# Reuse waits by tile, rope tables in a pool of their own, and gated weights fetched inside the attention, in a two-part transformer kernel

## The chip, the cores and the metric

The kernel runs on one core of a Trainium2 chip. Its time is the device time of one execution in microseconds. Engines are named as the profile names them: PE (TensorE, matrix products), PEld (its weight loads), DVE (VectorE), ACT (ScalarE), POOL (GpSimd), SP (SyncE, which here only issues DMAs). Each runs its own instructions in the order in which they were written down, and waits on the others by semaphores.

## The reference

Two residual sandwiches over x of shape 2 x 2048 x 256, in float32:

```python
x = x + layernorm(attn(layernorm(x)))   # compressed, selected and windowed attention, gated, 16 or so small products
x = x + layernorm(ffn(layernorm(x)))    # two layers, below

# one layer of ffn, 8 heads of 64, window 128
h = shift_token(x)                      # second half of the channels taken from the token before
q, k, v = split(h @ wqkv)
q, k = l2norm(q) * qs, l2norm(k) * ks
q, k = rotary_xpos(q, k)                # multiply by tables of cos and sin times a scale per position
x = x + local_attention(q, k, v) @ wo   # each block of 128 sees itself and the block before
h = layernorm(shift_token(x)) * lg + lb
a, g = split(h @ w1 + b1)
x = x + (a * gelu(g)) @ w2 + b2
```

## The kernel before, in words

The tokens are 32 tiles of 128 rows. Tensors X and Y hold them in SBUF throughout. **Part one** computes the first sandwich. Its instructions are noted down first and then given out in an order written out by hand (`FIRST`; line 150 of the profile is where they are given out). Its pools (`psum1`, `wa`, `big`, `work`, `tiny`) are then released. **Part two** computes the two layers. Each step is put on a list with a place, a number that stands for a due time in nanoseconds; the list is sorted by place and given out in that order (line 124 in the profile is the helper through which these instructions go). In both parts the order on each engine is the order of the program; nothing reorders it.

Pools of part two: `psum2` (PSUM banks, tags pa 2, pb 2, pc 4), `wf` (gated weights w1, w2, b2, the projection wo, the ring of keys KR, the inner activations U) and `act` (the tiles of the attention and of the gated stage). They are laid on the bytes and banks that part one's pools left. `wpool`, opened before part one's pools, holds wqkv and the scales qks; it takes over nothing.

The attention of a layer goes tile by tile, 32 tiles, alternating between the two sequences, 12,400 apart in place (`TILE`), each with 46 or so steps at fixed offsets (`PLACES`). The steps that matter here, for tile n:

- `table_load` (offset -20000, SP): for every second tile one DMA of 128 KB, a rope table `cs`; three buffers.
- `turn_input` (0, PE), `late_half` and `early_half` (ACT copies to `h`), `edge` (1424, POOL).
- `project` j = 1, 0, 2 (2265, 5394, 10688, PE): keys, queries, values, each into a pa bank, of which there are two.
- `square` (ACT), `table` (4442, POOL: cs times qks), `times` (8622 and 9762, DVE: projections times table, tile `rr`), `values` (ACT).
- `add`, `power`, `unit` (11152 to 18200, POOL: rotation and normalisation of rr), then `turn` (19662 and 20098, PE).
- `scores` (21969 and 29455, PE), softmax, `weigh`, `project_out` (49850, PE, which reads wo).

The gated stage of a layer overlaps the end of its attention; its first use of w1, w2, b2 and U in layer one is some 640 us into the span. `load_wo` issues one DMA on SP. `load_gated` issues a DMA on POOL (b2), a POOL memset, four DMAs on SP (w1), a second POOL memset, two DMAs on SP (w2); two of the w1 DMAs and the last w2 DMA write where a memset wrote. U's two tiles get a memset each on POOL.

In the kernel before, `fetch(0, "wo")`, `fetch(0, "gated")` and U's memsets stand ahead of the whole list, so they are the first instructions of part two on SP and POOL:

```python
    W[0]["wqkv"], W[0]["qks"] = attn_w
    fetch(0, "wo")
    fetch(0, "gated")
    begin = 0
```

Of the kernel before, what the change touches and what calls it, by code (L numbers as in the profile page):

```python
# [10 lines left out]
F32 = mybir.dt.float32  # L11
# [5 lines left out]
P = 128  # L17
# [11 lines left out]
DEPTH, HEADS, DH = 2, 8, 64  # L29
INNER = HEADS * DH  # L30
HID = int(H * 4 * 2 / 3)
NCH = -(-HID // P)
# [121 lines left out]
def sandwich_kernel(ctx: ExitStack, tc: tile.TileContext, x, Wq, bq, Wk, bk, Wv, bv, Wo, bo, Wg, bg,  # L154
                    Wc, bc, Ws, bs, wqkv, q_scale, k_scale, wo, ln_g, ln_b, w1, b1, w2, b2, rope, out):
    nc = Notes(tc.nc)
# [7 lines left out]

    def share(stack, name, **bufs):
        banks.update(bufs=bufs, pool=stack.enter_context(
            tc.tile_pool(name=name, bufs=1, space=bass.MemoryType.PSUM)))

    def bank(tag, shape):
        return later(banks["pool"], shape, F32, tag=tag, name=tag, bufs=banks["bufs"][tag])  # L170
# [16 lines left out]

    part1 = ExitStack()
    share(part1, "psum1", pa=3, pb=2, pc=2, po=1)


# [72 lines left out]
    wpool = ctx.enter_context(tc.tile_pool(name="wpool", bufs=1))  # L264

    def load_wqkv(l):
        a = wpool.tile([P, 2, 3 * INNER], F32, tag="wqkv", name=f"wqkv{l}")
        nc.cut()
        nc.sync.dma_start(a, wqkv[l].rearrange("(h p) n -> p h n", p=P))

        v = wpool.tile([P, 2, 2, DH], F32, tag="qks", name=f"qks{l}")
        for i in range(2):
            for j, sc in enumerate((q_scale[l], k_scale[l])):
                nc.cut()
                nc.sync.dma_start(v[:, i, j, :], sc.unsqueeze(0).to_broadcast([P, DH]))
        return a, v
# [601 lines left out]


    share(ctx, "psum2", pa=2, pb=2, pc=4)  # L880
    wf = ctx.enter_context(tc.tile_pool(name="wf", bufs=1))
    act = ctx.enter_context(tc.tile_pool(name="act", bufs=2))

    def load_wo(l):
        wo_s = wf.tile([P, INNER // P, H], F32, tag="wo", name=f"wo{l}")
        nc.sync.dma_start(wo_s, wo[l].rearrange("(h p) n -> p h n", p=P))
        return wo_s

    def load_gated(l):
        b2_b = wf.tile([P, H], F32, tag="b2", name=f"b2{l}")  # L890
        nc.gpsimd.dma_start(b2_b, b2[l].unsqueeze(0).to_broadcast([P, H]))


        a = wf.tile([P, 2, W1C], F32, tag="w1", name=f"w1{l}")
        w1v = w1[l].rearrange("(h p) n -> p h n", p=P)
        nc.gpsimd.memset(a[:, :, 2 * FULL :], 0.0)
        nc.sync.dma_start(a[:, :, 0:FULL], w1v[:, :, 0:FULL])
        nc.sync.dma_start(a[:, :, FULL : 2 * FULL], w1v[:, :, HID : HID + FULL])
        nc.sync.dma_start(a[:, :, 2 * FULL : 2 * FULL + REST], w1v[:, :, HID + FULL : 2 * HID])
        nc.sync.dma_start(a[:, :, 2 * FULL + HALF : 2 * FULL + HALF + REST], w1v[:, :, FULL:HID])  # L900
        o = wf.tile([P, NCH, H], F32, tag="w2", name=f"w2{l}")
        nc.gpsimd.memset(o[:, NCH - 1, :], 0.0)
        nc.sync.dma_start(o[:, 0 : NCH - 1, :], w2[l, 0:FULL, :].rearrange("(c p) n -> p c n", p=P))
        nc.sync.dma_start(o[0:REST, NCH - 1, :], w2[l, FULL:HID, :])
        return a, o, b2_b
# [5 lines left out]
    def put(place, f, *args):  # L911
        todo.append((place, len(todo), f, args))
# [26 lines left out]
    def attention(l, base):  # L939
        tabs = {}  # L940
        S = [dict() for _ in ORDER]

        def table_load(n):

            t, b = ORDER[n]
            if b == 0:
                tabs[t] = act.tile([P, 2, 2, DH], F32, tag="cs", name="cs", bufs=3)
                nc.sync.dma_start(tabs[t], rope[:, t].rearrange("p (i j) d -> p i j d", i=2))

        def table(n):  # L950
# [237 lines left out]

    U = [wf.tile([P, NCH, GT * P], F32, tag=f"u{i}", name=f"u{i}") for i in range(2)]
    for u in U:  # L1190
        nc.gpsimd.memset(u[:, NCH - 1, :], 0.0)

    def gated_units(l, base, no_gate_until, beside):
        G = {g: dict(u=U[i % 2]) for i, g in enumerate(GORDER)}
# [107 lines left out]
    def fetch(l, what):  # L1302
        if what == "wqkv":
            W[l]["wqkv"], W[l]["qks"] = load_wqkv(l)
        elif what == "wo":
            W[l]["wo"] = load_wo(l)
        else:
            W[l]["w1"], W[l]["w2"], W[l]["b2"] = load_gated(l)
# [1 line left out]


    W[0]["wqkv"], W[0]["qks"] = attn_w
    fetch(0, "wo")
    fetch(0, "gated")
    begin = 0
    for l in range(DEPTH):
        last_tile = begin + (len(ORDER) - 1) * TILE
# [60 lines left out]
```

## Time and profile before

| what | value |
|---|---|
| median of 3 runs | 1618.66 us (1618.02 to 1618.82) |
| the profiled execution | 1617.42 us, span 1615.7 us |
| mean granted PE clock | 0.976 |
| PE busy | 1530.9 us, 95% of the span |
| DVE, ACT, POOL busy | 66%, 47%, 45% |
| part one ends (last ACT instruction) | 241.0 us into the span |
| attention of layer one, PE full | 300 to 640 us, 339.98 of 340 busy |

The granted clock is the share of full speed that PE was given; at 0.50 a projection of 4 matmul records takes 3.4 us, at 1.00 it takes 1.7. Windows cut the span into stretches and give the busy time of each engine in each. A wait "A <- B" is idle time of A that ended when B did something. The timeline lists instructions in order of time; SPq and POOLq are the queues' own instructions.

### The profile page before, as it was taken

Reading aid. Unit: us, or ns where it says so; the run is one execution under the profiler, and the core shown is the slowest. Engines: PE = TensorE matmul, PEld = TensorE weight load, DVE = VectorE, ACT = ScalarE, POOL = GpSimd, SP = SyncE. Lnnn points to the kernel's source line nnn. Section 1 sums busy time; section 2 is a strip of 40 time slices with the busy share of each in tenths; the row PEclk is TensorE's granted clock in tenths of the full one; section 3 lists DMA queues with packets and bytes.
Section 4 is the critical chain, followed back from the end, with each engine's and each line's share of the span. In section 5 each row is a group of like instructions: output and inputs, shape, how many; then the busy total and the mean of one; then the engine's idle time right before and its main releaser. Section 6 shows DMA issues by size and latency. Waiting matters only on the chain.

```text
span 1615.7 us, 32188 instructions
## 1 busy us (share of the span) xinstructions
PE 1530.9 (95%) x12216; PEld 1013.0 (63%) x12216; DVE 1068.0 (66%) x3123; ACT 757.3 (47%) x2197; POOL 733.5 (45%) x906
## 2 busy tenths in 40 slices
PE   7999957999999999789999999999999987999998
PEld 6867743666666666546566556666666664656655
DVE  6588673788888888544445247888888884455543
ACT  5236652677676776411111147677676763111110
POOL 7114255666666666301111156666666661132332
PEclk9999987999999999899999999999999998999999
DMA  6000002000000000020000010000000000000000
GB/s 213 1 4 4 1 2 80 8 5 8 6 8 9 5 7 7 8 68 7 10 20 0 1 39 28 9 5 9 5 8 8 9 4 9 11 25 28 27 26 26
DMA packets 32389, 30.66 MB, mean 19 GB/s; under 512 B 5118, under 2 KB 30572, under 8 KB 32236
## 3 DMA queue, kind: packets, MB, share of 16 engines
q1 hardware_dynamic: 32044, 28.08, 5.7%
q8 instruction: 97, 1.59, 0.4%
q0 software_dynamic: 192, 0.52, 0.2%
q14 instruction: 56, 0.46, 0.1%
HBM read 20.21 MB, written 4.19 MB: 15 GB/s over the span
## 4 chain that ended last, share of the span: by engine, by line
PE 87%; DVE 5%; POOL 3%; DMA 3%; ACT 1%; issue 1%; SPq 0%; POOLq 0%; DVEq 0%; ACTq 0%
PE pa L124 30%; PE pb L124 23%; PE pc L124 23%; PE pa L150 5%; PE pc L150 3%; DMA sh<-Y 2%; PE pb L150 2%; PE po L150 1%; DVE prob L124 1%; POOL rr L124 1%; DVE rr L124 1%; DVE st L150 1%; POOL r L150 1%; DMA cs<-in_rope_dram 0%; POOL ss L124 0%
## 5 line engine op out<-in xcount | busy, mean ns | idle before, releaser
L124 PE MATMUL pa<-wqkv,h 128*128 128x512 f32 x768 | 377.6, 615 | 19.3 <-ACT h L124 9.9
L124 POOL TENSOR_TENSOR rr<-rr 128x256 f32<-128x256 f32 x256 | 178.0, 727 | 305.8 <-DVE rr L124 259.4
L124 ACT ACTIVATE ge<-pa,vb 128x512 f32<-128x512 f32 x92 | 63.1, 688 | 365.7 <-PE pa L124 360.3
L124 ACT ACTIVATE prob<-prob,off 128x192 f32<-128x192 f32 (+2 forms) x512 | 226.2, 445 | 11.9 <-DVE off L124 11.0
L124 PEld LDWEIGHTS pa<-wqkv,h 128*128 128x128 f32 x768 | 133.9, 194 | 134.7 <-issue 107.7
L124 POOL TENSOR_TENSOR ss<-ss,mhalf 128x16 f32<-128x16 f32 x64 | 188.0, 2937 | 3.3 <-DVE den L124 2.3
L124 ACT COPY probT<-pb 128x384 f32<-128x384 f32 (+1 forms) x256 | 119.9, 469 | 142.6 <-PE pb L124 139.6
L124 PE MATMUL pa<-hh,w 128*128 128x512 f32 x368 | 176.4, 609 | 5.3 <-ACT ge L124 5.3
L124 PE MATMUL pc<-w,u 128*128 128x256 f32 x768 | 175.7, 379 | 0.0
L124 PEld LDWEIGHTS pc<-w,u 128*128 128x128 f32 x768 | 145.8, 190 | 45.4 <-issue 28.7
L124 DVE CUSTOM_DVE_ANT_0 prob<-pc,mask_loc 128x192 f32<-128x192 f32 (+2 forms) x512 | 148.7, 346 | 25.9 <-PE pc L124 24.1
L124 DVE TENSOR_TENSOR rr<-pa,cs 128x1024 f32<-128x1024 f32 x128 | 150.6, 1216 | 21.6 <-POOL cs L124 14.0
L124 PE MATMUL pb<-hh,w 128*128 128x512 f32 x292 | 137.7, 594 | 0.0
L124 POOL TENSOR_SCALAR r<-mv 128x1 f32<-128x1 f32 (+1 forms) x48 | 11.2, 233 | 274.9 <-DVE mv L124 274.9
L124 POOL TENSOR_TENSOR rr<-rr,ss 128x512 f32<-128x512 f32 x128 | 132.9, 1058 | 2.3
L124 DVE TENSOR_TENSOR prob<-prob,den 128x768 f32<-128x768 f32 x128 | 128.0, 1000 | 4.9
L124 PE MATMUL pb<-wo,oT 128*128 128x256 f32 x512 | 124.8, 388 | 5.8 <-DVE oT L124 5.8
L124 PEld LDWEIGHTS pb<-ident,prob 128*128 128x128 f32 x752 | 89.2, 141 | 65.4 <-DVE prob L124 27.7
L124 PE MATMUL pb<-ident,prob 128*128 128x128 f32 x752 | 118.3, 279 | 11.2 <-DVE prob L124 9.4
L124 DVE SCALAR_TENSOR_TENSOR u<-pb,vb,ge 128x512 f32<-128x512 f32 x73 | 54.7, 750 | 105.6 <-PE pb L124 79.8
L124 ACT ACTIVATE sq<-pa 128x512 f32<-128x512 f32 x128 | 75.9, 593 | 97.0 <-PE pa L124 94.2
L124 PE MATMUL pc<-kr,qT 64*64 64x192 f32 (+2 forms) x2688 | 111.1, 289 | 3.4 <-ACT qT L124 3.4
(255 smaller groups left out, 2498.6 us busy)
## 6 DMA issues: line engine op xcount, KB each, us to landing
cs<-in_rope_dram SPq DMA_DIRECT2D x32, 128.0 KB
out_dram<-res SPq DMA_DIRECT2D x32, 128.0 KB
sh<-Y SPq DMA_DIRECT2D x16, 254.0 KB
w<-in_L_ffn_w_dram SPq DMA_DIRECT2D x6, 640.0 KB
X<-_attn_hidden_states_dram SPq DMA_DIRECT2D x7, 512.0 KB
wqkv<-in_L_ffn_wqkv_dram SPq DMA_DIRECT2D x2, 1536.0 KB
Wc<-in_L_attn_Wc_dram SPq DMA_DIRECT2D x1, 1024.0 KB
wo<-in_L_ffn_wo_dram SPq DMA_DIRECT2D x2, 512.0 KB
```

The source lines that it names most:

```text
L124: return f(*a, **k)
L150: f(*(now(x) for x in a), **{n: now(x) for n, x in k.items()})
```

## The change

Three things. The pools `psum2`, `wf` and `act` (and `psum1`, by the shared helper) are opened with `reuse_waits="tile"`: a tile that lands on bytes of released pools waits for the users of the tiles that lay on its own bytes (in PSUM, on its own bank), where before every tile of the pool waited for every user of the released pools. The rope tables move from `act` to `wpool`, still with three buffers. The load of wo, the load of the gated weights and U's memsets are put on the list at places 12000, 60000 and 61000.

```diff
     def share(stack, name, **bufs):
         banks.update(bufs=bufs, pool=stack.enter_context(
-            tc.tile_pool(name=name, bufs=1, space=bass.MemoryType.PSUM)))
+            tc.tile_pool(name=name, bufs=1, space=bass.MemoryType.PSUM, reuse_waits="tile")))
...
-    wf = ctx.enter_context(tc.tile_pool(name="wf", bufs=1))
-    act = ctx.enter_context(tc.tile_pool(name="act", bufs=2))
+
+    wf = ctx.enter_context(tc.tile_pool(name="wf", bufs=1, reuse_waits="tile"))
+    act = ctx.enter_context(tc.tile_pool(name="act", bufs=2, reuse_waits="tile"))
...
-                tabs[t] = act.tile([P, 2, 2, DH], F32, tag="cs", name="cs", bufs=3)
+                tabs[t] = wpool.tile([P, 2, 2, DH], F32, tag="cs", name="cs", bufs=3)
...
-        nc.gpsimd.memset(u[:, NCH - 1, :], 0.0)
+        put(61000, nc.gpsimd.memset, u[:, NCH - 1, :], 0.0)
...
-    fetch(0, "wo")
-    fetch(0, "gated")
+    put(12000, fetch, 0, "wo")
+    put(60000, fetch, 0, "gated")
```

## The prediction

> **What bounds the kernel now.** I read the page first, then the windows over the hand-over from the first to the second part, then the waits there, then the timeline. The page says that TensorE is the bound:
>
> ```profile
> PE 1530.9 (95%) x12216; PEld 1013.0 (63%) x12216; DVE 1068.0 (66%) x3123; ACT 757.3 (47%) x2197; POOL 733.5 (45%) x906
> ```
>
> So only what shortens a hole in PE, or work done at half clock, can pay. From 300 to 640 us the windows give PE 339.98 of 340 us busy at clock 1.00: a time gained before 300 is kept to 640. The diff acts at the hand-over, so I cut that into 3.4 us slots (columns: stretch, length, busy of PE, PEld, DVE, ACT, POOL, then granted clock, DMA share, GB/s):
>
> ```profile
> 240.70:244.10 3.40, 2.57 (x3) 1.00 (x4) 0.00 (x0) 0.74 (x3) 2.20 (x6) 0.50 0.59 155
> 244.10:247.50 3.40, 3.40 (x5) 1.35 (x4) 0.00 (x0) 0.60 (x1) 0.00 (x0) 0.50 1.06 331
> 247.50:250.90 3.40, 0.74 (x2) 0.00 (x0) 0.00 (x0) 0.60 (x1) 0.00 (x0) 0.99 0.99 294
> 250.90:254.40 3.50, 0.00 (x0) 0.00 (x0) 0.56 (x1) 0.00 (x0) 0.72 (x1) 0.51 0.47 141
> 254.40:257.80 3.40, 2.68 (x3) 1.18 (x4) 3.28 (x4) 0.00 (x0) 1.52 (x3) 0.50 0.00 0
> 257.80:261.20 3.40, 2.88 (x6) 1.29 (x5) 0.00 (x0) 0.93 (x3) 3.40 (x4) 0.50 0.00 0
> 261.20:264.60 3.40, 3.40 (x5) 1.34 (x5) 0.29 (x1) 0.60 (x1) 2.81 (x3) 0.50 0.00 0
> 264.60:268.00 3.40, 2.62 (x27) 1.58 (x26) 2.37 (x3) 1.57 (x3) 0.13 (x1) 1.00 0.00 0
> ...
> 274.80:278.30 3.50, 1.89 (x10) 0.84 (x8) 3.18 (x4) 1.47 (x5) 2.66 (x4) 0.99 0.00 0
> 278.30:281.70 3.40, 2.86 (x20) 1.99 (x21) 2.06 (x3) 1.47 (x6) 2.74 (x5) 0.50 0.00 0
> ```
>
> Two things are to be seen. PE is empty from 248.2 to 255.1 while the DMA moves 300 GB/s. And the clock of a slot follows how full PE was in the slot before: 3.40 of 3.40 gives 1.00 next, 2.57 to 2.88 leaves 0.50 at 0.50, 1.89 of 3.50 drops 1.00 to 0.50. What PE waited for, from the waits of 240 to 300 us (total, times, longest):
>
> ```profile
> DVE rr L124 <- POOL cs L124: 14.0, 1, 14.0
> POOL cs L124 <- DMA cs<-in_rope_dram: 9.8, 1, 9.8
> PE pa L124 <- DVE rr L124: 6.9, 1, 6.9
> ```
>
> The third projection of tile 0 (`project`, part 2) needs a pa bank that `times` has to empty; `times` needs the table cs, scaled on POOL; the table needs its DMA. The timeline says why that is late:
>
> ```profile
> 241.03 0.38 SPq L124 DMA_DIRECT2D wo<-in_L_ffn_wo_dram  x1
> 241.04 0.44 ACT L124 COPY h<-pb 128x128 f32<-128x128 f32 x2
> 241.46 3.68 SPq L124 DMA_DIRECT2D w<-in_L_ffn_w_dram  x6
> 241.53 6.71 PE L124 MATMUL pa<-wqkv,h 128*128 128x512 f32 x8 [7.46 <-ACT h L124]
> 245.25 1.48 SPq L124 DMA_DIRECT2D cs<-in_rope_dram  x3
> ```
>
> SP issued its last load of part one at 32.5 and then waited 207 us for part one to end; only behind wo and six gated weights came the tables, which landed at 252.9.
>
> **The change, part by part.**
>
> *Waits by tile.* ACT runs in order and ends part one's last `Y<-X` at 241.01; the h copy follows at 241.04. So the wait by tile moves neither it nor PE's start at 241.53: gain 0. PE's first transposes may move from 233.38 to 232.7, under cover of that same wait: 0. POOL ends part one at 239.7; the edge memset (0.12) leaves 243.15 for 241.0 or earlier.
>
> *Tables in wpool.* They take over no old bytes, and at place -20000 and 4800 they stand ahead of wo: the first two are issued at about 33 us and have landed long before 241. The scaling (0.73) is done by about 241.9. `times` then waits for the square alone: the first runs 246.07 to 247.29 (square 245.44 + 0.60), the second 248.90 to 250.13 (square 248.28 + 0.60), instead of 253.84 to 256.20.
>
> *What is late next.* I replay the fill with the durations of the timeline:
> - PE: tile 0's third projection now at 247.9, at clock 1.00 (the full slot before it grants that), 4 x 0.43: to 249.65. Tile 1's transposes 0.38, copies and hand-over 0.6, its two projections 3.46: to 254.1.
> - POOL: from the end of `times` to the end of `unit` before is 256.20 to 264.09, 7.9 us (adds 2.77, power 2.92, units 2.04). Now 250.13 + 7.9 = 258.0, the first unit 1.0 earlier.
> - So PE has nothing from 254.1 to 257.0: **the hole shrinks and moves to `unit`**. That slot is a quarter full; the next runs at 0.50, and since it fills to about 80% the one after too. Slow: key and query turns to 259.05, qT copy, scores 259.75 to 260.95, values of tile 1 (3.4) to 264.35, transposes of tile 2 (0.64) to 264.95.
> - Fast again: tile 2's first projection 265.5 to 267.2, scores 0.65, second projection to 269.6, tile 1's turns to 270.5 (its units done at 267.9, not late), scores at 271.2, tile 2's values at 272.1, tile 3's first projection at 275.0. Before, that began at 285.05, after a slow stretch from 278.3 to 285.1 that now has no cause.
> - POOL is the limit once more: `times` of tile 2 ends at 273.3, and its units, which took 278.96 to 289.05 before with 1.4 us of waits in it, end at 273.4 + 8.8 = 282.2. PE ends tile 2's turns at 282.7 instead of 290.86: **8.1 us**. After this PE had no waits before and I expect none.
>
> *The clock rule.* The row comes first: 1.89 us of work in a 3.50 us slot was enough for 0.50 in the next, and a start at 241.53 became fast at 247.5 only. The Trainium skill, "TensorE: Matmul & The Clock Gate", Part 1 (The HAM clock gate), has the clock fall after at least one idle window of about 3.4 us. By that, a pause of 2.9 us costs nothing: values of tile 1 take 1.73 for 3.4, and the fill comes out at 10.8 us. I take the rows' 8.1.
>
> *Gated weights and u at 60000 and 61000.* On POOL the fetch is one b2 DMA (0.64) and two memsets of w (0.58 together); it falls behind tile 3's units (place 55400) and ahead of tile 4's adds (60752), where POOL waited 3.89 us:
>
> ```profile
> 299.75 2.05 POOL L124 TENSOR_TENSOR rr<-rr,ss 128x512 f32<-128x512 f32 x2
> 305.69 2.79 POOL L124 TENSOR_TENSOR rr<-rr 128x256 f32<-128x256 f32 x4 [3.89 <-DVE rr L124]
> ```
>
> 1.2 in 3.9: 0. The two u memsets (0.99) come between tile 4's adds; the units then end 1.0 later, where they had 0.8 to 0.9 us before PE's turns at 313.5 and 314.4: a loss of **0.2**. Uncovered, all 2.2 us would show. A rule that speaks against this: "SBUF — State Buffer", in "SBUF: two separate sides", has POOL fully blocked, descriptors for its DMAs too, while DVE runs a two-port operation. The trace's DMA issue took 0.642 beside an idle DVE and 0.647 in the second layer's attention, but DVE was idle for most of that one too, so the rows don't refute it. By the rule one DVE operation (up to 1.2, `rr`) more: 2.4 in 3.9, still 0; with a second one, 3.6, still inside.
>
> *SP's queue.* The gated weights' last pieces follow a POOL memset, so SP stands until about 292, and behind it the table of tile 8. That one is scaled at about 341 now (12.5 us a tile); 2.1 MB at the 300 GB/s seen are 7 us: 40 us to spare. wo, ahead of tile 4's table, waits till 241 at most; the table is needed near 290. Issuing costs PE nothing. The 2.1 MB now fall into full attention: in the second layer, with the DMA at 347 GB/s from 970 to 972, PE was 2.00 of 2.00 busy: 0.
>
> *More waits in instructions.* The trace doesn't show them; gaps of POOL's queue around its waits are 0.04 each. Below: 0, as they can be over before 241. Above: some twenty first uses of tiles between 241 and 282, 0.8 us. Taken: 0, nearest to what the copy at 241.04 shows, 0.03 after its predecessor.
>
> **Sum.** Profiled execution 1617.42 (span 1615.7 and 1.7 around it) - 8.1 + 0.2 = 1609.5. The median of the runs stands 1.24 above that execution; 1618.66 - 7.9 = 1610.76, said as **1610.7**.
>
> **Rivals.**
> - *The clock stays up* (the page's rule, or slots that fall otherwise): 10.8 gained less 0.2, 1608.1. For: a slot half full, 1.99 of 3.40 at 210, kept 1.00. Against: the 1.89 above.
> - *More slow slots*: each costs 1.7 us, half of 3.4. Two more in the fill or at 640 to 720: 1614.1. For: the slots' edges fall elsewhere once the work is shifted.
> - *The change doesn't do what it says*: the waits by tile could be ignored for some pool. The tables would still be early, in a pool that takes over nothing, so 1610.7 stands; only if SP still held them behind old users would it be 1618.7.
> - *Slower*: the layer change (640 to 720) and the start of the last gated stage (1330 to 1390) each hold about five slow slots, 17 us, with fast ones between. A shift of 8 us moves their edges. With 1.7 us a slot, 7 more than before turn the gain into a loss of over 0.2%: 8 more give 1624. Against: full slots restore the clock by themselves.
>
> **How the numbers follow.** The likeliest 0.68; clock stays up 0.10; more slow slots 0.10; no effect 0.04; slower 0.08. The first three are faster by over 0.2% (3.2 us, about what a measurement of this kernel can tell): 0.88; same 0.04; slower 0.08. The likeliest one's own range is 1608.5 to 1613; with clock and slots on both sides 1606.5 to 1615.0, which leaves out no effect, slower and a little.
>
> **What would show it.** Tables issued near 33 us; `times` of tile 0 beginning near 246.1 with no wait for cs; PE's hole before its third projection gone, one of about 3 us before tile 0's turns; tile 3's first projection near 275; tile 2's turns done near 282.7; the six w loads near 291. Wrong if PE starts part two away from 241.5, if POOL's chain is not what PE waits for, or if a wait appears between 290 and 640.

## The result

| | before | after |
|---|---|---|
| median of 5 runs each, same chip | 1618.66 us (1615.83 to 1619.02) | 1610.11 us (1607.32 to 1610.5) |
| profiled execution, its span | 1617.42, 1615.7 us | 1610.34, 1608.6 us |
| mean granted PE clock | 0.976 | 0.980 |
| PE busy | 1530.9 us | 1525.9 us |

The ratio is 0.9947, with an interval of 0.9932 to 0.9961: 8.55 us less. It was 1610.7 that was forecast. The change was timed again later (e10 below): 0.9966 (0.9955 to 0.9977), 5.0 us. Why the gain itself moves is one of the findings below.

The bound is the same; the first two lines of the page after:

```profile
span 1608.6 us, 32178 instructions
...
PE 1525.9 (95%) x12216; PEld 1012.2 (63%) x12216; DVE 1068.5 (66%) x3123; ACT 754.7 (47%) x2197; POOL 734.9 (46%) x906
```

SP's queue after (start, duration, operation, count; a row with a long duration holds a wait):

```profile
31.33 1.00 SPq L124 DMA_DIRECT2D cs<-in_rope_dram  x2
225.96 0.38 SPq L124 DMA_DIRECT2D wo<-in_L_ffn_wo_dram  x1
226.38 32.54 SPq L124 DMA_DIRECT2D cs<-in_rope_dram  x2
258.97 35.55 SPq L124 DMA_DIRECT2D w<-in_L_ffn_w_dram  x6
```

The first two tables are issued 200 us before they are used, and the gated weights no longer stand at the hand-over.

The waits after, from 240 to 300 us (total, times, longest). The three lines that the prediction showed are gone; these stand in their place:

```profile
POOL rr L124 <- DVE rr L124: 17.8, 4, 9.3
...
DVE rr L124 <- ACT sq L124: 10.4, 4, 6.2
...
PE pb L124 <- POOL rr L124: 2.8, 4, 1.1
...
PE pa L124 <- POOL h L124: 1.4, 2, 0.9
```

`times` (DVE rr) now waits for the square alone, and no wait of PE on POOL is longer than 1.1 us. The windows after, over the same stretches as in the prediction (columns as there):

```profile
240.70:244.10 3.40, 0.81 (x1) 0.50 (x2) 0.71 (x1) 2.01 (x5) 0.94 (x3) 0.50 0.00 0
244.10:247.50 3.40, 3.40 (x6) 1.38 (x5) 0.00 (x0) 0.39 (x1) 0.00 (x0) 0.54 0.00 0
247.50:250.90 3.40, 3.23 (x8) 1.17 (x7) 2.54 (x3) 0.81 (x2) 0.00 (x0) 1.00 0.00 0
250.90:254.40 3.50, 2.12 (x7) 0.80 (x6) 1.45 (x2) 0.92 (x3) 3.45 (x6) 1.00 0.00 0
254.40:257.80 3.40, 2.26 (x7) 0.71 (x5) 1.72 (x2) 1.19 (x2) 3.32 (x3) 1.00 0.00 0
257.80:261.20 3.40, 2.33 (x25) 1.54 (x26) 2.79 (x8) 1.17 (x2) 3.40 (x5) 1.00 0.38 93
...
278.30:281.70 3.40, 2.12 (x17) 1.01 (x19) 2.85 (x4) 1.66 (x6) 2.59 (x4) 1.00 0.00 0
```

The empty stretch is gone, and from 247.2 to 650 the clock stays at 1.00, where before six slots of the fill ran at 0.50. But PE starts part two later than before, as the timeline of the hand-over after shows:

```profile
240.92 0.73 POOL L124 TENSOR_TENSOR cs<-cs,qks 128x256 f32<-128x256 f32 x1
240.95 0.71 DVE L150 SCALAR_TENSOR_TENSOR CLOSE<-mv,CLOSE 128x2 f32<-128x2 f32 x1 [0.89 <-POOL h L124]
241.69 1.09 ACT L150 ACTIVATE Y<-X,CLOSE 128x256 f32<-128x256 f32 x2 [0.51 <-DVE CLOSE L150]
242.81 0.43 ACT L124 COPY h<-pb 128x128 f32<-128x128 f32 x2
...
243.29 5.62 PE L124 MATMUL pa<-wqkv,h 128*128 128x512 f32 x8 [8.89 <-ACT h L124]
...
247.81 1.23 DVE L124 TENSOR_TENSOR rr<-pa,cs 128x1024 f32<-128x1024 f32 x1 [6.16 <-ACT sq L124]
```

Part one's last CLOSE on DVE takes 0.71 us; the one before it took 0.16. It ends at 241.66 with POOL's table product at 241.65, which the free table has let in there. The last `Y<-X`, the copy and PE follow it.

**Where the 7 us of the profiled pair came from.** Both kernels issue the same 12,216 PE matmul records in the same order, so the start of the n-th can be subtracted (my arithmetic on the traces, each counted from the start of its own span, as the timelines are; the first profile of before is the zero). The table has this for all runs. "Start" is the first projection of part two, "fill" the gain from there to the scores right behind tile 2's turns, "U" the loss from there until after U's memsets, "rest" everything later. "End" is the last matrix product; it differs from the zero as the spans do. Minus is earlier, in us.

| run | start | fill | U | rest | end |
|---|---|---|---|---|---|
| after | +1.76 | -11.13 | +1.06 | +1.23 | -7.08 |
| e1 tables only | +2.28 | -10.91 | +0.07 | +2.15 | -6.42 |
| e2 order only | -0.27 | -10.92 | +1.06 | +1.42 | -8.71 |
| e3 waits by tile only | -0.26 | -9.39 | +0.07 | +2.02 | -7.57 |
| e4 U early | +0.12 | -11.06 | +0.07 | -1.36 | -12.24 |
| e5 edge early | +0.22 | -9.02 | +0.92 | +2.31 | -5.56 |
| e6 no waits by tile | +1.48 | -11.01 | +1.06 | +1.31 | -7.16 |
| e7 order, U early | -0.35 | -11.00 | +0.06 | -1.28 | -12.57 |
| e8 units delayed | -0.30 | -7.92 | +0.07 | -0.30 | -8.45 |
| e10 change again | -0.14 | -9.77 | +1.06 | -0.90 | -9.75 |
| e11 U early again | +1.76 | -10.31 | +0.07 | +2.52 | -5.95 |
| e12 no waits, U early | -0.28 | -10.85 | +0.06 | +2.06 | -9.01 |
| e13 before again | +1.18 | -3.47 | -0.01 | +0.97 | -1.33 |

### The profile page after: what moved, and what is told of

The parts are those of the page before. It is cut to its first block, busy times and chain, and to the rows that moved or that the text cites. A ratio compares the mean times of both kernels' runs of the same rounds, so it can differ in the third digit from the quotient of the medians.

```text
span 1608.6 us, 32178 instructions
## 1 busy us (share of the span) xinstructions
PE 1525.9 (95%) x12216; PEld 1012.2 (63%) x12216; DVE 1068.5 (66%) x3123; ACT 754.7 (47%) x2197; POOL 734.9 (46%) x906
## 4 chain that ended last, share of the span: by engine, by line
PE 74%; DVE 4%; POOL 2%; DMA 2%; ACT 1%; issue 1%; SPq 0%; POOLq 0%; DVEq 0%; ACTq 0%
PE pa L124 28%; PE pb L124 23%; PE pc L124 22%; DMA sh<-Y 2%; DVE prob L124 2%; POOL rr L124 1%; DVE rr L124 1%; POOL ss L124 1%; ACT prob L124 0%; DVE hh L124 0%; DVE st L124 0%; DVE ss L124 0%; DVE Y L124 0%; ACT L124 0%; DVE oT L124 0%
## 5 line engine op out<-in xcount | busy, mean ns | idle before, releaser
L124 PE MATMUL pa<-wqkv,h 128*128 128x512 f32 x768 | 371.6, 606 | 16.5 <-ACT h L124 11.6
L124 POOL TENSOR_SCALAR r<-mv 128x1 f32<-128x1 f32 (+1 forms) x48 | 11.1, 232 | 276.1 <-DVE mv L124 276.1
```

Of the source, the lines that this page charges most:

```text
L124: return f(*a, **k)
```

## The experiments

Diffs are against the changed kernel unless said otherwise. The first four ran on one chip beside the kernel before at 1616.32 us, the next four beside 1617.13, the next three beside 1614.05, the last beside 1615.44. Two theories stood at the outset: that SP's order (the gated load out of the way) gives the gain, or that the tables' buffers, which take over nothing, give it by themselves.

**e1, the tables alone.** Waits by tile off, fetches and U's memsets back ahead of the list:

```diff
-    put(12000, fetch, 0, "wo")
-    put(60000, fetch, 0, "gated")
+    fetch(0, "wo")
+    fetch(0, "gated")
```

> Only the tables move to wpool; waits by pool, and wo and the gated weights stay first on SP. Theory (the first table is late because it stands behind wo and six gated loads in SP's queue): SP still stands until 241, the tables are issued near 245, PE's hole before tile 0's third projection stays at about 6.9 us, time 1618.7 within 1.5. Rival (buffers that take over nothing are what counts): tables near 33 us, about 1610.

Measured 1608.25 us, 0.9956 (0.9941 to 0.9971): the theory missed, the full gain is there. SP's queue in this kernel:

```profile
31.25 1.42 SPq L124 DMA_DIRECT2D cs<-in_rope_dram  x3
243.31 0.38 SPq L124 DMA_DIRECT2D wo<-in_L_ffn_wo_dram  x1
243.74 4.06 SPq L124 DMA_DIRECT2D w<-in_L_ffn_w_dram  x6
```

In the program's text the fetches come first, in the trace the tables do, 212 us ahead of them. So the section on the kernel before is wrong where it says that nothing reorders part two. The order written out for part one and the list of part two stand inside `with tc.manual_schedule()` in the kernel; the two fetches stand outside both, and here they came out behind the three free tables. Nothing else moved: PE, DVE, ACT and POOL have the order of the kernel before, instruction for instruction. As an edit, the buffers that take over nothing are enough. But e1 changed SP's order too; what free tables gain behind waiting loads was not run.

**e2, the order alone.** Fetches and memsets at 12000, 60000 and 61000; tables in `act`, no waits by tile:

```diff
-                tabs[t] = wpool.tile([P, 2, 2, DH], F32, tag="cs", name="cs", bufs=3)
+                tabs[t] = act.tile([P, 2, 2, DH], F32, tag="cs", name="cs", bufs=3)
```

> Only the order moves (wo at 12000, gated weights at 60000, u at 61000); tables stay in act, all pools wait as before. Theory (SP's order is the cause): the table is issued at 241.0 as SP's first, lands near 244 and is scaled by 245, ahead of the square's end at 246.1; the whole gain, 1609 to 1611.5. Also DVE's last CLOSE step of part one keeps its 0.16 us, since POOL's table product comes later. Rival (waits by tile are what frees the start): no gain, 1618.7.

Measured 1608.43, 0.9954 (0.9941 to 0.9967), as the theory had it. The tables are SP's first issue of part two, at 240.77, and POOL has one early enough:

```profile
243.45 0.72 POOL L124 TENSOR_TENSOR cs<-cs,qks 128x256 f32<-128x256 f32 x1 [2.55 <-DMA cs<-in_rope_dram]
```

`times` needs it at 245.77, when the square is done: 1.6 us to spare. Either part gives the whole gain; together they give it once.

**e3, the waits by tile alone.** All pools by tile; tables in `act`, fetches and memsets first.

```diff
-        put(61000, nc.gpsimd.memset, u[:, NCH - 1, :], 0.0)
+        nc.gpsimd.memset(u[:, NCH - 1, :], 0.0)
```

> Only the three pools wait by tile; order and tables as before. Theory: SP can issue wo and the first gated loads once their own bytes are free, some 15 us earlier, but the last four gated loads follow POOL's memsets, which come behind part one's last POOL step, both u memsets and the b2 DMA (240 + 2.2), so the tables are issued near 244.3 and land near 247; times begins near 248 instead of 246.1: about 2 us of the gain missing, 1612 to 1613.5. Rival (waits by tile are all of it): 1610. Rival (waits do nothing alone): 1618.7.

Measured 1610.88, 0.997 (0.9962 to 0.9978), 5.4 us less where the theory had 5.2 to 6.7. wo goes out at 224.82, but the six gated pieces hold SP until 243.50, and POOL gets the table late:

```profile
247.51 0.72 POOL L124 TENSOR_TENSOR cs<-cs,qks 128x256 f32<-128x256 f32 x1 [5.93 <-DMA cs<-in_rope_dram]
```

`times` begins at 248.26, and the fill gains 9.39 instead of some 11. The waits help in this order of SP; they aren't the best way. Of the changed versions e3 alone keeps SP's order, with the tables behind the gated loads; in e1, e2 and the change the tables stand ahead of them, and the fill gains 10.9 to 11.1. So it is their place in SP's queue that the full gain goes with.

**e4, U's memsets ahead of the adds.**

```diff
-        put(61000, nc.gpsimd.memset, u[:, NCH - 1, :], 0.0)
+        put(56000, nc.gpsimd.memset, u[:, NCH - 1, :], 0.0)
```

> The changed kernel with u's two memsets at 56000 instead of 61000, so that they fall into POOL's idle gap ahead of tile 4's adds. Theory: the step of 1.05 us by which PE falls back between 300 and 307 us is the memsets between the adds; it goes, and PE's wait for the edge step there with it; 1609.1. Rival: the memsets cost about 1 us wherever they stand in the attention, 1610.1.

Measured 1606.31, 0.9945 (0.9927 to 0.9963). In the change the memsets cut tile 4's adds in two. Its timeline:

```profile
297.75 0.97 POOL L124 MEMSET u<- 128x512 f32 x2
...
298.70 1.40 POOL L124 TENSOR_TENSOR rr<-rr 128x256 f32<-128x256 f32 x2
...
299.97 0.96 DVE L124 TENSOR_TENSOR prob<-prob,den 128x768 f32<-128x768 f32 x1
300.05 0.93 POOL L124 COPY h<-h 128x1 f32<-128x1 f32 x1
...
301.03 1.13 PE L124 MATMUL pa<-wqkv,h 128*128 128x512 f32 x2 [0.45 <-POOL h L124]
```

The adds end late, the edge copy behind them falls beside a DVE multiply and takes 0.93, and PE waits for it; the rest comes with the units, late too. With place 56000 the memsets fall into POOL's idle time (timeline of e4):

```profile
289.87 0.99 POOL L124 MEMSET u<- 128x512 f32 x2
...
294.81 2.79 POOL L124 TENSOR_TENSOR rr<-rr 128x256 f32<-128x256 f32 x4 [2.78 <-DVE rr L124]
297.55 0.18 POOL L124 COPY h<-h 128x1 f32<-128x1 f32 x1
```

POOL still has 2.78 us of idle time, the copy takes 0.18, and the step of 1.06 in the table falls to 0.06.

**e5, the edge early.** In the change, tile 1's edge memset stands behind tile 0's adds, and PE waits for it (timeline after):

```profile
253.65 0.09 POOL L124 MEMSET h<- 128x1 f32 x1
...
253.80 2.84 PE L124 MATMUL pa<-wqkv,h 128*128 128x512 f32 x6 [0.85 <-POOL h L124]
...
257.78 0.66 PE L124 MATMUL pb<-ident,rr 128*128 128x128 f32 x4 [1.14 <-POOL rr L124]
```

The edit moves it ahead (the allocation of `h1` moves with it):

```diff
-("early_half", 1155), ("edge", 1424),
+("early_half", 1155), ("edge", -1500),
```

> The changed kernel with the step edge at offset -1500 instead of 1424 (it takes the buffer for h1), so that tile 1's edge memset no longer stands behind tile 0's adds on POOL. Theory (POOL's chain of adds, power and units sets the fill): PE's wait of 0.85 us for it goes, its hole before tile 0's turns grows from 1.1 to about 2.0, and tile 2's turns end where they did: 8.5 us faster than before, as the change. If the forecast's reading of the clock holds (a slot about half empty drops the next to 0.50), the wider hole brings two slow slots, and only 5 to 6 us are left. Rival (the edge wait itself costs 0.85): 9.4 us faster than before.

Measured 1612.42, 0.9979 (0.997 to 0.9989). The wait of 0.85 is gone and the fill gains only 9.02. PE ran ahead of POOL, and the hole before tile 0's turns grew from 1.14 to 2.29:

```profile
256.27 2.11 PE L124 MATMUL pb<-ident,rr 128*128 128x128 f32 x8 [2.29 <-POOL rr L124]
```

The windows of e5, cut where its own clock changes:

```profile
249.20:252.60 3.40, 2.88 (x9) 1.28 (x8) 1.66 (x3) 1.23 (x4) 3.14 (x5) 1.00 0.00 0
252.60:256.00 3.40, 1.38 (x4) 0.31 (x2) 2.58 (x3) 0.89 (x2) 3.32 (x2) 1.00 0.00 0
256.00:259.40 3.40, 2.40 (x18) 1.72 (x21) 1.21 (x2) 1.17 (x2) 3.40 (x7) 0.50 0.64 181
259.40:262.80 3.40, 3.40 (x19) 1.61 (x14) 1.06 (x9) 0.00 (x0) 3.40 (x2) 0.50 0.64 248
```

A slot with 1.38 of 3.40 busy is followed by one at 0.50; 2.40 there isn't enough, so a second follows; 3.40 ends it. That is the pattern that the prediction had drawn for the change, met here with a hole of 2.29.

**e6, without the waits by tile.** Tables in `wpool` and the new order stay.

```diff
-    act = ctx.enter_context(tc.tile_pool(name="act", bufs=2, reuse_waits="tile"))
+    act = ctx.enter_context(tc.tile_pool(name="act", bufs=2))
```

(`wf` and the PSUM pools likewise.)

> The changed kernel without the waits by tile: tables in wpool, order moved, all pools wait as before. Theory (they bring nothing here, and let POOL's first table product into the tail of part one, where DVE's last CLOSE step takes 0.71 instead of 0.16): that step takes 0.16 again, PE starts part two about 0.5 us earlier after its transposes than in the changed kernel; 8.5 to 9.5 us faster than before. Rival (they carry part of the gain): less than 8.

Measured 1609.6, 0.9954 (0.9937 to 0.997), 7.5 us less. That is in the rival's range, below 8, but the interval reaches from 4.8 to 10.2 us and doesn't decide. The table does: the fill gains 11.01 without the waits by tile and 11.13 with them, so they carry nothing of it, and the difference from the theory lies in the start and the rest. The table product comes behind the last CLOSE:

```profile
241.21 0.16 DVE L150 SCALAR_TENSOR_TENSOR CLOSE<-mv,CLOSE 128x2 f32<-128x2 f32 x1 [0.89 <-POOL CLOSE L150]
...
242.76 0.72 POOL L124 TENSOR_TENSOR cs<-cs,qks 128x256 f32<-128x256 f32 x1
...
243.01 5.44 PE L124 MATMUL pa<-wqkv,h 128*128 128x512 f32 x7 [7.45 <-ACT h L124]
```

From the start of CLOSE to PE's first projection are 1.80 us here and 2.34 in the change.

**e7, the order alone with U early.** e2 with U's memsets at 56000.

```diff
-        put(61000, nc.gpsimd.memset, u[:, NCH - 1, :], 0.0)
+        put(56000, nc.gpsimd.memset, u[:, NCH - 1, :], 0.0)
```

> Only the order moves, with u's memsets at 56000: no waits by tile, tables in act. Theory: it takes the fill's 10.9 us, loses neither the 1.0 at the memsets nor the 0.5 in part one's tail: PE 10.9 us ahead from 320 to 640 us relative to where it starts part two, the fastest of all, 9.5 to 11 us faster than before. Rival (order alone leaves something): slower than the changed kernel.

Measured 1607.36, 0.9946 (0.9928 to 0.9963), 9.8 us less, as the theory had it; its profiled execution took 1604.82, the shortest of all.

**e8, POOL's chain lengthened.** e7 with three memsets before tile 0's units. It was built with U at 56000, so e7 is what it stands against:

```diff
+    for i in range(3):
+        put(17190, nc.gpsimd.memset, U[0][:, NCH - 1, :], 0.0)
```

> Only the order moves, and POOL has three more memsets of 0.52 us ahead of tile 0's units (they write a part of u that is zeroed again later). A dose on what the prediction took for the next limit. Theory (POOL's chain sets the fill): the hole before tile 0's turns grows from 1.1 to 2.7 us and the fill's gain falls by 1.6 to about 9.3; if a slot half empty then drops the clock, by 2 to 3 more, to about 7. Rival (PE's own work sets the fill, POOL has slack): no loss, 10.9.

Measured 1610.3, 0.996 (0.9946 to 0.9974). The hole before the turns is 2.66, and the windows of e8, at its own edges, show one slow slot:

```profile
252.70:256.10 3.40, 2.18 (x6) 0.64 (x4) 1.78 (x2) 1.19 (x2) 3.28 (x4) 1.00 0.00 0
256.10:259.50 3.40, 1.31 (x8) 0.84 (x8) 2.38 (x3) 0.85 (x2) 3.40 (x5) 1.00 0.41 101
259.50:262.90 3.40, 3.03 (x19) 1.67 (x20) 1.06 (x9) 0.32 (x1) 3.40 (x5) 0.50 0.86 328
```

The fill gains 7.92 against e7's 11.00: of these 3.1 us, 1.68 are the memsets (their row on POOL), and the remaining 1.4 are near what one slow slot can cost, 1.7. The theory had 9.3, or about 7 with slow slots; the rival, no loss, is out. So POOL's chain sets PE's time in the fill, and a longer hole costs more than its length.

**e10, e11, e12: three versions side by side.** The change again; with U at 56000 (e4's edit); with U at 56000 and no waits by tile (e6's edit too).

```diff
-        put(61000, nc.gpsimd.memset, u[:, NCH - 1, :], 0.0)
+        put(56000, nc.gpsimd.memset, u[:, NCH - 1, :], 0.0)
```

> The change as it is, beside the two versions that follow, so that the three are compared with each other. Theory: 0.9947 of the kernel before again, about 8.5 us; in its trace PE loses 0.5 us at the start of part two (the table product on POOL beside part one's last DVE CLOSE) and 1.0 us at U's memsets. Rival: these two losses are made up elsewhere, so that all three kernels agree within 0.3 us.

> The change with U's memsets at place 56000 instead of 61000. Theory: 1.0 us below the change, the loss at U's memsets. Rival: the same time as the change within 0.3 us, because clock slots at the layer changes scatter by more than that between executions.

> The change with U's memsets at place 56000 and without the waits by tile (tables still in wpool). Theory: the 0.5 us at the start of part two is gone as well, 1.5 us below the change and the fastest of the three. Rival: equal to the version with the early memsets alone, if the later start of the transposes costs what the table product does.

Measured 1609.05, 1609.01 and 1608.74; ratios 0.9966, 0.9964, 0.9965, each within 0.0012. The rival holds: within about 0.3 us they are one. The step at U is there in e10's trace and absent in e11's and e12's, just as the theory says, but e11 lost 2.52 later while e10 gained 0.90. On medians neither e4 nor e7 has been shown to beat the change.

e10 is also the change's second profile, and its fill gains 9.77 instead of 11.13. The hole before tile 0's turns is the same (1.15 against 1.14), but here its slot, 254.9 to 258.3, had 1.64 of 3.40 busy, and the next one ran at 0.50.

**e13, the kernel before once more** (no edit).

> The kernel before, profiled in a second execution, since its median went from 1618.66 to 1614.05 us over four groups of runs while the change's moved from 1610.11 to 1609.05. Theory: the hole at 248 to 255 us and the slow slots up to 285 us come again, so that the end of tile 2's turns is within 1.5 us of 290.86, and what differs are slow slots at 640 to 720 and 1330 to 1400 us. Rival: the slots of the fill itself fall otherwise, and the fill ends 2 us or more earlier than in the first profile, so that the gain of 11 us there is in part the first profile's luck.

Measured 1615.1 us beside 1615.44; profiled execution 1616.06. The rival holds again: tile 2's turns ended 2.28 earlier than in the first profile (at 288.58), though part two had begun 1.18 later. Its windows at its own edges:

```profile
250.40:253.80 3.40, 0.00 (x0) 0.00 (x0) 0.00 (x0) 0.00 (x0) 0.00 (x0) 1.00 0.95 312
253.80:257.20 3.40, 1.02 (x2) 0.51 (x3) 2.30 (x3) 0.00 (x0) 0.72 (x1) 0.50 0.01 5
257.20:260.60 3.40, 3.19 (x6) 1.11 (x4) 1.53 (x3) 0.18 (x2) 3.27 (x6) 0.50 0.00 0
260.60:264.00 3.40, 3.09 (x7) 1.44 (x8) 0.44 (x1) 1.34 (x4) 3.32 (x2) 1.00 0.00 0
```

The hole is the same (PE waited 7.62 for `times`), but after it the edges lay so that one slot was nearly full at once and the clock rose at 260.6; in the first profile slots with 2.68 and 2.88 kept it down until 264.6. So of the 11 us that the fill gains against the first profile, 3.5 are how that execution's slots fell: the first profile has six at 0.50 between 250 and 290, this one three. Against this one the change's first profile gains 7.7, and its second 6.3.

## Why the prediction was right, and where only the sum was

The mechanism is the forecast one: the tables' transfers were late, `times` stood behind them, PE behind `times`, and the gain of the fill is kept to 640 us (offset -8.30 after U's memsets, -8.17 at 631). That the total came so near is in part luck: misses of opposite sign met. Of the prediction's own signs of being wrong two came, PE's start away from 241.5 and a wait between 290 and 640 (0.45 at 301, for the edge copy); what PE waits for in the fill was named rightly. Against the first profile, step by step:

- **Tables at 33 us:** 31.33. Right. (SP's wait before, given as 207 us, is 208.5, from 32.5 to 241.03; nothing rests on it.)
- **PE starts part two at 241.53, "the wait by tile moves neither it" (0):** wrong, 243.29. Of the 1.76 late, about 0.55 belong to the change: POOL's product beside DVE's CLOSE. The five kernels with both waits by tile and tables in `wpool` (after, e4, e5, e10, e11) show it; in e6 and e12, which differ in the waits alone, the product comes after CLOSE. The rest, 1.2, was lost in part one at 220 to 228 us, ahead of anything that the change touches: two slots ran at 0.50 there from 219.9, where the first profile of before had one. The kernel before lost as much in its second profile (+1.18), again with two.
- **`times` at 246.07, no wait for cs:** 247.81, the square alone ahead of it. Right but for the late start.
- **"The hole shrinks and moves to `unit`", 2.9 us:** it moved there, with 1.14. POOL's price was right: 6.9 us from the end of `times` (250.81) to the first unit's end (257.7), as forecast. What was missed is PE's side. Its projections ended at 256.64 and not 254.1: 1.76 late at the start, and the edge memset of tile 1 behind tile 0's adds, 0.85. I had replayed POOL's adds, power and units, but not what its queue holds for the next tile.
- **Two slow slots behind the hole:** none came. The slots with holes in them had 2.02, 2.64 and 1.94 of 3.40 busy and all kept 1.00. That isn't a victory of the rule of the Trainium skill, "TensorE: Matmul & The Clock Gate", Part 1 (The HAM clock gate), by which the clock falls after at least one idle window of about 3.4 us: e5 and e8 had no such window, their pauses were 2.29 and 2.66, and the clock fell. The reading of the rows holds, the hole was mis-sized. Where the slots' edges fall counts too: e10, the same kernel with the same hole, has one slow slot behind it.
- **Fill 8.1 us:** 11.1 against the first profile. The rival "the clock stays up" had 10.8, so its number fits, though not its reason. With a second profile of each kernel it lies between 6.3 and 11.1, and 8.1 is inside: the term was measured against one throw of the dice, which no step of the prediction said. In plain time, tile 3's first projection began at 273.24 (forecast 275.0) and tile 2's turns ended at 281.6 (282.7), for all the late start.
- **Gated load in POOL's pause, 0; the last w loads near 291:** their issue ended at 294.5, behind POOL's memsets, which ended at 292.7. Late by 3, and it cost nothing that shows: e11 and e12 hold that load in the same pause, with no step.
- **U's memsets 0.2:** 1.0. The step asked only for the units' slack and left out the edge copy behind the same adds. The Trainium skill, "SBUF — State Buffer", "SBUF: two separate sides", says that a POOL instruction that reads SBUF is fully blocked while a DVE operation with two SBUF inputs runs; I weighed that for the DMA issue, where it cost nothing, and not for this copy, where the trace agrees with it (0.93, ended at 300.98 with DVE's multiply at 300.93).
- **Everything kept after 640:** 1.15 of it was lost at the layer change (640 to 720). "Rest" in the table lies between -1.36 and +2.52 over kernels whose instructions there are the same, and it is +0.97 for the kernel before itself. It goes with where slots fall; what sets their phase was not tried.

By the terms: +1.76 - 11.13 + 1.06 + 1.23 = -7.08, against a forecast of -8.1 + 0.2 = -7.9 for the profiled execution. "The change doesn't do what it says" is out, since SP issued the tables early. "Slower" needed seven more slow slots; the mean clock rose.

## What to carry to other kernels

A load that is needed at a hand-over should write into bytes that nobody used before, or be first in its queue behind it: either edit alone was worth the whole gain here, and both put the tables ahead of the gated loads. When a stall is removed, replay the next engine's queue with all that it holds, the small memsets and copies for the next tile too, since 0.1 us of work can stand behind 2.8. And price a gain against more than one profile of the kernel before: when idle time drops the clock, one execution's slots can be worth 3.5 us in 50.

## What the runs showed of the hardware

- **Clock slots.** Cut at each execution's own edges (about 3.41 us apart), slots with 1.31 (e8), 1.38 (e5), 1.64 (e10), 1.89 (before) and even 1.97 (e1 and e10, near 210.6 in part one) of 3.40 busy dropped the next from 1.00 to 0.50, while slots with 1.64 (e7, at 651.7), 1.79 (e8), 1.94 and 2.02 (after) kept it. Over all the traces no slot below 1.57 kept it and none above 1.98 lost it; between the two both occur, so busy time alone doesn't draw the border. From 0.50, slots of part two with up to 2.89 (before) didn't bring it back, and slots with 2.98 (e7) or more did; in part one a slot with 3.39 (e6, at 220.1) didn't, so there too busy time isn't all.
- **POOL and DVE block each other over tiny operands.** A CLOSE of 128x2 took 0.71 instead of 0.16 on DVE beside POOL's table product; an edge copy of 128x1 took 0.93 instead of 0.18 on POOL beside DVE's multiply. Each ended within 0.05 us of the other engine's instruction.
- **Executions differ without any change.** The median of the kernel before was 1614.05 to 1618.66 over the groups of runs, that of the change 1609.05 and 1610.11. The later groups ran on four different chips, but the spread is there on one too: beside e10, 26 executions of the kernel before took 1610.78 to 1618.22.
